# Edge weights of two tiles as one product over 128 partitions: a map stored twice and padded with zeros

## The chip, the core and the metric

The kernel runs on one NeuronCore of a Trainium2 chip. A core has five engines that run on their own and wait for each other by semaphores: TensorE (PE; loads of its stationary operand are shown apart as PEld), VectorE (DVE), ScalarE (ACT), GpSimd (POOL) and SyncE (SP). Tables and inputs lie in HBM; tiles that are worked on lie in SBUF, 128 partitions wide; matrix products are written to PSUM. The metric is the time of one execution on the device in microseconds (us); less is better.

## The reference, cut to what matters

A graph layer over 12,500 nodes with 160 features each and 400,000 edges that are sorted by destination, with a residual and a layer norm. What the change touches is `w`, the weights that each edge gets from its 64 numbers:

```python
h_s = s @ lin1_ws * a * _inv(S_IN)
h_v = jnp.einsum('nci,cd->ndi', v, lin1_wv) * a[:, :, None] * _inv(V_IN)
hid = jax.nn.silu(edge_scalars @ fc_w1 * _inv(R))      # 400000 x 64
w = hid @ fc_w2 * _inv(FC_HID)                          # 400000 x 224
w1, w2, w3, w4, w5 = jnp.split(w, [64, 128, 160, 192], axis=-1)
es = h_s[edge_src]
ev = h_v[edge_src]
...
agg_s = jax.ops.segment_sum(mid_s, edge_dst, num_segments=n) * inv_nn
agg_v = jax.ops.segment_sum(mid_v, edge_dst, num_segments=n) * inv_nn
...
return jnp.concatenate([scalars, gated.reshape(n, 3 * V_OUT)], axis=-1)
...
x = _layernorm(x + _L0_gnn_ref(x, node_vec1, src, dst, edge_attr_4, edge_attr_64, ...))
```

`mid_s` and `mid_v` are products of `w`, of the gathered rows `es` and `ev`, and of the four numbers of the edge. All of it is float32.

## The kernel before, in words

A first part maps all nodes by `lin1` and writes the rows to a table `h_tab` in HBM. Then the edges are worked on in tiles of 128, 3,125 of them. 24 tiles are a chunk, and a chunk has two halves of 12: the first half's edge numbers lie on partitions 0 to 63 of the tile `es`, the second half's on partitions 64 to 127. A step takes a quad of four tiles, two of the one half and two of the other; there are 782 steps (the last one has one tile). The order of the work on every engine is written out by the loop over `steps` (lines 994 to 1063), and each engine takes its instructions in that order.

A step n issues, engine by engine:

- POOL: four gathers of 128 rows each from `h_tab` into `hg` (L476), 160 numbers a row. The third of them carries a wait for the edge weights of step n - 3 (`pace`, lines 1010 and 1011), so that gathers don't run further ahead than that. Six buffers of `hg` are there.
- PE: the edge weights `pw` of the step's four tiles (L551), and then the sums `pa` of step n - 2 (L630), a one-hot product that adds each edge to its destination in a window of 16 nodes; the sums of the two halves go to PSUM partitions 0 to 63 and 64 to 127. In every second step PE also makes `hid` for two later quads (L467: all 128 partitions of `es`, 512 columns), about every third step it turns sums around (L649), about every twelfth it maps them by `lin2` (L664), and for every four tiles of nodes it finishes nodes (L717, L721).
- DVE: the one-hot (L614, written into the free columns of `pw`), the products of `pw` and `hg` (L561, L569), the one-hot times the edge's four numbers (`sel`, L623), and the additions of finished windows into `acc` (L672).
- ACT: the silu of `hid` (L469), and copies out of PSUM.

There are two PSUM buffers of `pw`, two banks each, so the weights of step n wait until DVE has read those of step n - 2.

The edge weights of one tile are a product of `hid` (64 partitions by 128 edges, the stationary operand) and the map `w2` (64 partitions by 224, the moving operand). `w2` stands on partitions 0 to 63 and again on 64 to 127, each half taking the copy on its own partitions. The four products of a quad are issued in the order half 0, half 1, half 0, half 1, so that neighbours lie on different halves of the partitions and write to different PSUM banks. Each float32 product appears in the profile as two loads and two matmuls (6,250 of each for 3,125 tiles).

Lists that are read by slot (`rel`, `eas`) are laid out once in the order in which the quads take their tiles: `by_slots` (L171), `by_slot` (L588), `quads` (L121).

Of the kernel before, what the change touches and what calls it, by code (L numbers as in the profile page):

```python
# [10 lines left out]
F32 = mybir.dt.float32  # L11
# [10 lines left out]
P = 128  # L22
S = 64
# [12 lines left out]
CT = 2 * SIDE  # L36
# [12 lines left out]
NWT = 224  # L49
# [12 lines left out]
def gnn_kernel(  # L62
# [21 lines left out]
    nc = tc.nc  # L84
# [10 lines left out]
    consts = ctx.enter_context(tc.tile_pool(name="consts", bufs=1))  # L95
# [25 lines left out]
    def quads(halves):  # L121
        out = []
        for t in range(0, max(halves), 2):
            out.append([(half, u) for half in range(2) for u in range(t, t + 2) if u < halves[half]])
        return out


# [12 lines left out]
    for c, (_, halves) in enumerate(chunks):  # L140
        for i, slots in enumerate(quads(halves)):
            steps.append((c, i, [(tile_of(c, half, u), half, u) for half, u in slots]))
# [7 lines left out]
    def ahead(t):  # L150
        a0 = t // AHEAD * AHEAD
        if a0 not in aheads:
            n = min(AHEAD, TT - a0)
            idx = loads.tile([P, AHEAD], I32, name="idx")
            eat = loads.tile([P, AHEAD, 4], F32, name="eat", bufs=1)
            k = 0
            while k < n:
                g, u = divmod(a0 + k, GT)
                m = min(n - k, GT - u)
                nc.sync.dma_start(idx[:, k:k + m], src[g][:, u:u + m])  # L160
                nc.sync.dma_start(eat[:, k:k + m].rearrange("p t k -> p (t k)"),
                                  ea[g].rearrange("p t k -> p (t k)")[:, 4 * u:4 * (u + m)])
                k += m
            aheads[a0] = a0, idx, eat
        return aheads[a0]
# [5 lines left out]
    def by_slots(out, of, n, f):  # L171


        m = n // CT
        for u in range(SIDE if m else 0):
            at = u // 2 * 4 + u % 2
            o, i = out[:, at:at + 1], of[:, u:u + 1]
            f(bass.AP(tensor=o.tensor, offset=o.offset,
                      ap=[o.ap[0], [CT * o.ap[1][0], m], [2 * o.ap[1][0], 2], *o.ap[2:]]),
              bass.AP(tensor=i.tensor, offset=i.offset,  # L180
                      ap=[i.ap[0], [CT * i.ap[1][0], m], [SIDE * i.ap[1][0], 2], *i.ap[2:]]),
              u // BT, m)
        return m * CT
# [36 lines left out]
    w1 = consts.tile([2 * S, 2 * S], F32, name="w1")  # L220
    nc.vector.memset(w1, 0.0)

    w2 = consts.tile([2 * S, NWT], F32, name="w2")
    l2 = consts.tile([P, 11, V3], F32, name="l2")
    nc.vector.memset(l2, 0.0)
    share = ends_pool.tile([1, NB], I32, name="share")
# [10 lines left out]
    with tc.tile_pool(name="nodes", bufs=len(starts)) as nodes, tc.tile_pool(  # L237
        name="nodes_ps", bufs=6, space=PSUM
# [33 lines left out]
        for q in range(4):  # L272
            t0, s = divmod(q * QN, P)
            nc.gpsimd.dma_start(at_k[:P - s, q], attr[s:, t0:t0 + NQ])
            if s:
                m = min(NQ, NT - t0 - 1)
# [8 lines left out]
        at = ends_pool.tile([P, NT], F32, name="at")  # L285
# [8 lines left out]
        halves = ends_pool.tile([P, 2], F32, name="halves")  # L294
# [32 lines left out]
        raw = ends_pool.tile([2 * S, NWT], F32, name="raw")  # L327
        for half in range(2):
            r = slice(half * S, (half + 1) * S)
# [14 lines left out]
        for c0, cn, xw, xz in loaded:  # L344
# [7 lines left out]
            n = min(cn, P)  # L352
# [32 lines left out]
    nc.vector.tensor_scalar_mul(half_at, at, 0.5)  # L385
    iota = consts.tile([P, W], F32, name="iota")
    nc.vector.tensor_copy(iota, iota_i)
    at_c = 0
    for a, b in ((64, 128), (0, 64), (192, 224), (160, 192), (128, 160)):
        nc.vector.tensor_scalar_mul(w2[:, at_c:at_c + b - a], raw[:, a:b], 1.0 / math.sqrt(64))  # L390
        at_c += b - a

    scs = consts.tile([S, V3], F32, name="scs")
    nc.sync.dma_start(scs, sc_ws)
# [14 lines left out]
    for to, part, pieces, w, r0, c0, by in maps:  # L409
        for k, piece in enumerate(pieces):  # L410
# [3 lines left out]
            m = terms.setdefault((to, part, four), len(terms))  # L414
            at_r = at_p * V
            r = l2[at_r:at_r + V, m, c0:c0 + w.shape[1]]
# [11 lines left out]
    for t in range(by_slots(rel, dt, TT, relative), TT):  # L428
        nc.vector.tensor_tensor(rel[:, slot_of[t]:slot_of[t] + 1], dt[:, t:t + 1],  # L429
                                lo[:, t // BT:t // BT + 1], op=OP.subtract)  # L430
# [27 lines left out]
    def hidden(pool, psum, es, halves, t0, n):  # L458

        ph = psum.tile([2 * S, Q * P], F32, name="ph", tag="misc")  # L460
        hid = pool.tile([2 * S, Q * P], F32, name="hid", bufs=3)
        ends = [max(0, min(n, m - t0)) for m in halves]
        assert ends[0] >= ends[1]
        for k, c0, c1 in ((2 * S, 0, ends[1]), (S, ends[1], ends[0])):
            if c1 > c0:
                c = slice(c0 * P, c1 * P)
                nc.tensor.matmul(ph[:k, c], w1[:k, :k], es[:k, t0 * P + c0 * P:t0 * P + c1 * P],  # L467
                                 start=True, stop=True)
                nc.scalar.activation(hid[:k, c], ph[:k, c], AF.Silu, scale=1.0 / math.sqrt(64))  # L469
        return hid  # L470
# [73 lines left out]
    weighed, summed = [], []  # L544

    def weights(psum, hid, slots):

        pw = psum.tile([P, Q, 256], F32, name="pw")
        for t, (half, c) in sorted(enumerate(slots), key=lambda k: (k[1][1], k[1][0])):
            r = slice(half * S, (half + 1) * S)  # L550
            weighed.append(nc.tensor.matmul(pw[:, t, :NWT], hid[r, c * P:(c + 1) * P], w2[r],  # L551
                                            start=True, stop=True).ins.name)
        return pw

    def products(pool, pw, hg, n, between=None):
# [32 lines left out]
    def by_slot(t):  # L588

        a0, _, eat = ahead(t)  # L590
        if a0 not in sorted_eat:
            n = min(AHEAD, TT - a0)
            eas = loads.tile([P, AHEAD, 4], F32, name="eas")
            m = n // CT
            for u in range(0, SIDE if m else 0, 2):
                o, i = eas[:, 2 * u:2 * u + 1], eat[:, u:u + 1]
                nc.scalar.copy(
                    bass.AP(tensor=o.tensor, offset=o.offset,
                            ap=[o.ap[0], [4 * CT, m], [4, 2], [8, 2], [1, 4]]),
                    bass.AP(tensor=i.tensor, offset=i.offset,  # L600
                            ap=[i.ap[0], [4 * CT, m], [4, 2], [4 * SIDE, 2], [1, 4]]))
            m *= CT
            for k in range(m, n):
                o = slot_of[a0 + k] - a0
                nc.scalar.copy(eas[:, o], eat[:, k])
            sorted_eat[a0] = eas
        return sorted_eat[a0]
# [172 lines left out]
    with tc.tile_pool(  # L780
        name="fin", bufs=1
    ) as fin, tc.tile_pool(
        name="mine", bufs=2
    ) as mine, tc.tile_pool(
        name="late", bufs=2
    ) as late, tc.tile_pool(name="edge", bufs=2) as edge, tc.tile_pool(
        name="deep", bufs=6
# [199 lines left out]
        with in_order:  # L987
# [6 lines left out]
            for n, (c, i, tiles) in enumerate(steps):  # L994
# [11 lines left out]
                if n == 0:  # L1006
# [61 lines left out]
            n = len(steps)  # L1068
# [29 lines left out]
        with tc.For_i(0, n_redo, 1):  # L1098
# [9 lines left out]
            with tc.For_i(0, n_again, 1) as g, tc.For_i(0, GT, 1) as k:  # L1108
                t = g * GT + k
# [97 lines left out]
```

## Time and profile before

| | |
|---|---|
| median of 3 runs | 4658.97 us (4657.78 to 4659.96) |
| the profiled execution | 4659.28 us, its span 4657.5 us |
| mean granted TensorE clock | 0.870 |
| PE busy | 3852.9 us, 17,955 matmuls |
| PE weight loads | 1891.7 us, 17,955 loads |
| POOL busy | 2995.5 us, of it 2964.8 us in 3,125 gathers |
| DVE busy | 2369.7 us |
| ACT busy | 840.2 us |

The span runs from the first to the last instruction of the core; the execution's own time is 1.8 us longer. In the groups by line, a row gives the line of the kernel, the engine, the operation, what is written and read, its shape and how often; behind the bar stand the busy time, the mean duration of one in ns, and the time that the engine idled just before them, with what ended most of that idle time ("issue": nothing that the profile shows). Busy time of PE is counted with the tail of each matmul, and the next one starts before that tail ends; the chain of work that ended last counts each piece only up to the start of the next.

### The profile page before, as it was taken

The page shows a single profiled execution, that of the slowest core. Times are in us where ns is not written, and L with a number is a line of the kernel's source. Part 1 is how long each engine was busy: PE and PEld are TensorE (multiplying, and loading weights), DVE is VectorE, ACT ScalarE, POOL GpSimd, SP SyncE. Part 2 cuts the span into 40 slices and gives each one's busy share as a digit, 9 for nine tenths or more (in the row PEclk, how much of TensorE's full clock was granted, in tenths as well). Part 3 has the DMA queues.
Part 4 walks back from the last instruction along what each step waited for, and adds up shares of the span by engine and source line. Part 5 has one row for each costly group of instructions (what it writes and reads, how often), then busy time and mean ns, then how long its engine had stood idle before and what let it go on. Part 6 is the DMA issues. An engine that isn't in the chain of part 4 may idle for free.

```text
span 4657.5 us, 53879 instructions
## 1 busy us (share of the span) xinstructions
PE 3852.9 (83%) x17955; PEld 1891.7 (41%) x17955; DVE 2369.7 (51%) x6412; ACT 840.2 (18%) x1872; POOL 2995.5 (64%) x3172
## 2 busy tenths in 40 slices
PE   5788888888888888888888888887888888888886
PEld 4343444444444334344443444343443444444443
DVE  5544554545545455454554555554554554554454
ACT  1211121211111111111111111111111111111112
POOL 6666666666666666666666666666666666666663
PEclk8888898888888898888888888888888898988888
DMA  6333333333333333333333333333333333333331
GB/s 208 93 79 79 95 86 81 94 78 88 95 78 89 87 84 88 90 84 86 90 85 85 89 88 85 89 87 79 93 88 79 93 80 87 95 78 88 86 87 48
DMA packets 237510, 412.26 MB, mean 89 GB/s; under 512 B 78040, under 2 KB 160961, under 8 KB 237093
## 3 DMA queue, kind: packets, MB, share of 16 engines
q0 software_dynamic: 152960, 266.64, 21.8%
q1 hardware_dynamic: 83668, 141.96, 12.5%
q8 instruction: 143, 2.34, 0.2%
q14 instruction: 145, 1.19, 0.1%
q10 hardware_dynamic: 594, 0.13, 0.0%
HBM read 392.49 MB, written 16.00 MB: 88 GB/s over the span
## 4 chain that ended last, share of the span: by engine, by line
PE 63%; issue 12%; another core or an unknown queue 10%; DVE 9%; DMA 2%; POOL 2%; ACT 1%; DVEq 0%; SPq 0%; ACTq 0%; POOLq 0%
PE pa L630 23%; PE pw L551 17%; PE misc L664 8%; PE misc L467 7%; PE misc L649 6%; DVE pr L569 5%; POOL hg L476 2%; PE misc L721 2%; DMA hg<-h_tab,idx 1%; DVE sel L623 1%; PE misc L717 1%; DVE pr L561 1%; DVE pw L614 1%; DMA xz<-in_xv_t_dram 1%
## 5 line engine op out<-in xcount | busy, mean ns | idle before, releaser
L476 POOL DMA_INDIRECT hg<-h_tab,idx x3125 | 2964.8, 949 | 1601.1 <-issue 824.7
L630 PE MATMUL pa<-pr,sel 128*64 128x416 f32 x6250 | 1546.6, 585 | 122.8 <-issue 118.5
L551 PE MATMUL pw<-w,hid 64*128 64x224 f32 x6250 | 1050.7, 408 | 382.9 <-issue 257.7
L614 DVE TENSOR_TENSOR pw<-rel,iota 128x64 f32<-128x64 int16 x782 | 180.1, 230 | 2143.1 <-remote 1114.7
L569 DVE TENSOR_TENSOR pr<-pw,hg 128x384 f32<-128x384 f32 x2346 | 1153.2, 547 | 0.0
L551 PEld LDWEIGHTS pw<-w,hid 64*128 64x128 f32 x6250 | 644.2, 203 | 1078.8 <-issue 742.1
L630 PEld LDWEIGHTS pa<-pr,sel 128*64 128x64 f32 x6250 | 444.4, 149 | 971.3 <-issue 924.5
L561 DVE TENSOR_TENSOR pr<-pw,hg 128x512 f32<-128x512 f32 x782 | 540.2, 691 | 30.3 <-DVE pw L614 1.9
L467 PE MATMUL misc<-es,w 128*128 128x512 f32 (+1 forms) x784 | 491.3, 709 | 30.5 <-DVE rel L429 19.6
L664 PE MATMUL misc<-tt,l 128*96 128x256 f32 (+5 forms) x1496 | 400.3, 411 | 42.8 <-issue 40.6
L469 ACT ACTIVATE hid<-misc 128x512 f32<-128x512 f32 x392 | 234.4, 598 | 977.3 <-remote 277.7
L652 ACT COPY tt<-misc 128x512 f32<-128x512 f32 (+1 forms) x263 | 153.0, 582 | 1426.5 <-remote 826.8
L863 ACT COPY sa<-pa 128x416 f32<-128x416 f32 x521 | 263.9, 507 | 714.2 <-remote 279.9
L649 PE MATMUL misc<-ident,sa 128*128 128x128 f32 (+1 forms) x1558 | 311.3, 290 | 76.6 <-ACT sa L863 42.3
L623 DVE TENSOR_TENSOR sel<-pw,eas 128x256 f32<-128x256 f32 x782 | 323.2, 413 | 0.1
L664 PEld LDWEIGHTS misc<-tt,l 128*96 128x96 f32 (+1 forms) x1496 | 241.9, 176 | 194.9 <-issue 125.9
L649 PEld LDWEIGHTS misc<-ident,sa 128*128 128x128 f32 x1558 | 218.5, 173 | 162.2 <-issue 100.5
L672 DVE TENSOR_TENSOR acc<-acc,os 96x32 f32 x1042 | 194.1, 186 | 53.4 <-remote 16.3
L467 PEld LDWEIGHTS misc<-es,w 128*128 128x128 f32 x784 | 129.3, 205 | 157.3 <-issue 131.7
L649 PE MATMUL misc<-first_last,sa 128*128 128x128 f32 x784 | 188.8, 297 | 4.3 <-issue 4.2
L717 PE MATMUL misc<-ident,acc 96*128 96x96 f32 x196 | 64.0, 332 | 95.7 <-DVE pw L614 68.3
L667 ACT COPY os<-misc 96x512 f32<-96x512 f32 (+2 forms) x68 | 38.4, 564 | 449.9 <-PE misc L664 168.7
(97 smaller groups left out, 852.1 us busy)
## 6 DMA issues: line engine op xcount, KB each, us to landing
es<-in_es_t_dram SPq DMA_DIRECT2D x258, 384.0 KB
hg<-h_tab,idx POOLq DMA_INDIRECT x3125
h_tab<-ht POOLq DMA_DIRECT2D x24, 320.0 KB
xt<-in_x_dram SPq DMA_DIRECT2D x23, 320.0 KB
out_dram<-y SPq DMA_DIRECT2D x23, 320.0 KB
xv<-in_xv_t_dram SPq DMA_DIRECT2D x23, 192.0 KB
eat<-in_ea_dram SPq DMA_DIRECT2D x41, 96.0 KB
xw<-in_xs_t_dram SPq DMA_DIRECT2D x6, 512.0 KB
```

The source lines that it names most:

```text
L467: nc.tensor.matmul(ph[:k, c], w1[:k, :k], es[:k, t0 * P + c0 * P:t0 * P + c1 * P], start=True, stop=True)
L469: nc.scalar.activation(hid[:k, c], ph[:k, c], AF.Silu, scale=1.0 / math.sqrt(64))
L476: got = nc.gpsimd.indirect_dma_start(out=hg[:, t, :], out_offset=None, in_=h_tab, in_offset=bass.IndirectOffsetOnAxis(ap=i, axis=0))
L551: weighed.append(nc.tensor.matmul(pw[:, t, :NWT], hid[r, c * P:(c + 1) * P], w2[r], start=True, stop=True).ins.name)
L561: nc.vector.tensor_mul(two, pw[:, :n, :2 * S].rearrange("p t (k c) -> p t k c", k=2), hg[:, :n, None, :S].to_broadcast([P, n, 2, S]))
L569: nc.vector.tensor_mul(pr[:, :n, first:first + V3].rearrange("p t (i c) -> p t i c", i=3), pw[:, :n, None, 2 * S + k * V:2 * S + (k + 1) * ...
L614: nc.vector.tensor_tensor(oh, rel[:, t0:t0 + n, None].to_broadcast([P, n, W]), iota[:, None, :].to_broadcast([P, n, W]), op=OP.is_equal)
L623: nc.vector.tensor_mul(sel[:, :n], oh[:, :, None, :].to_broadcast([P, n, 4, W]), by_slot(tiles[0][0])[:, u:u + n, :, None].to_broadcast([P ...
L630: summed.append(nc.tensor.matmul(pa[half * ROWS:(half + 1) * ROWS, :NPR], sel[:, t].rearrange("p k w -> p (k w)"), pr, start=start, stop=s ...
L649: nc.tensor.matmul(to.rearrange("p (k b w) -> p k b w", k=kinds, b=n), of, moving, start=True, stop=True, is_transpose=kinds == 4)
L664: nc.tensor.matmul(po[:, k, :nb], l2[r, terms[to, part, four]], a[:, :nb], start=(n == 0), stop=(n == len(of) - 1))
L863: nc.scalar.copy(sa, pas.pop(j)[:, :NPR])
```

## The change

The map `w2` gets a second block of 224 columns: partitions 0 to 63 hold the map in the first block and zeros in the second, partitions 64 to 127 zeros in the first and the map in the second. One product then takes `hid` on all 128 partitions, the tiles of both halves at the same place u, and all 448 columns: its first 224 columns are the weights of the first half's tile, the other 224 those of the second half's. A quad has two such products in place of four. So that the two tiles of a product lie side by side in `pw`, the quad's slots are ordered by place and then by half; before, they were ordered by half. `rel` and `eas` are laid out in that order. The last step, with one tile, uses 64 partitions and 224 columns as before.

```diff
         for t in range(0, max(halves), 2):
-            out.append([(half, u) for half in range(2) for u in range(t, t + 2) if u < halves[half]])
+            out.append([(half, u) for u in range(t, t + 2) for half in range(2) if u < halves[half]])
         return out
...
-    w2 = consts.tile([2 * S, NWT], F32, name="w2")
+    w2 = consts.tile([2 * S, 2, NWT], F32, name="w2")
+    nc.vector.memset(w2, 0.0)
...
-    at_c = 0
-    for a, b in ((64, 128), (0, 64), (192, 224), (160, 192), (128, 160)):
-        nc.vector.tensor_scalar_mul(w2[:, at_c:at_c + b - a], raw[:, a:b], 1.0 / math.sqrt(64))
-        at_c += b - a
+    for half in range(2):
+        r = slice(half * S, (half + 1) * S)
+        at_c = 0
+        for a, b in ((64, 128), (0, 64), (192, 224), (160, 192), (128, 160)):
+            nc.vector.tensor_scalar_mul(w2[r, half, at_c:at_c + b - a], raw[r, a:b], 1.0 / math.sqrt(64))
+            at_c += b - a
...
     def weights(psum, hid, slots):
 
         pw = psum.tile([P, Q, 256], F32, name="pw")
-        for t, (half, c) in sorted(enumerate(slots), key=lambda k: (k[1][1], k[1][0])):
-            r = slice(half * S, (half + 1) * S)
-            weighed.append(nc.tensor.matmul(pw[:, t, :NWT], hid[r, c * P:(c + 1) * P], w2[r],
-                                            start=True, stop=True).ins.name)
+        n = len(slots)
+        for t in range(0, n, 2):
+            half, c = slots[t]
+            m = min(2, n - t)
+            assert half == 0 and all(slots[t + k] == (k, c) for k in range(m))
+            weighed.append(nc.tensor.matmul(
+                pw[:, t:t + m, :NWT], hid[:m * S, c * P:(c + 1) * P], w2[:m * S, :m],
+                start=True, stop=True).ins.name)
         return pw
...
-                            ap=[o.ap[0], [4 * CT, m], [4, 2], [8, 2], [1, 4]]),
+                            ap=[o.ap[0], [4 * CT, m], [8, 2], [4, 2], [1, 4]]),
```

In the loop the order of PE stays, and only the rows of `pw` change. Two steps of PE in the middle of the program, before (`misc` are the PSUM banks for all else, `w_93` is `fc_w1` on the diagonal, `w_95` is `w2`):

```order
L630 MATMUL pa_513<-pr,sel 64x416 x4
L551 MATMUL pw_512<-w_95,hid 128x224 x4
L467 MATMUL misc_515<-es,w_93 128x512
L630 MATMUL pa_513<-pr,sel 64x416 x2
L630 MATMUL pa_514<-pr,sel 64x416 x2
L551 MATMUL pw_511<-w_95,hid 128x224 x4
L649 MATMUL misc_516<-ident,sa 128x128 x2
```

The same place after the change:

```order
L636 MATMUL pa_519<-pr,sel 64x416 x4
L556 MATMUL pw_518<-w_95,hid 128x2x224 x2
L469 MATMUL misc_521<-es,w_93 128x512
L636 MATMUL pa_519<-pr,sel 64x416 x2
L636 MATMUL pa_520<-pr,sel 64x416 x2
L556 MATMUL pw_517<-w_95,hid 128x2x224 x2
L655 MATMUL misc_522<-ident,sa 128x128 x2
```

Four products of 224 columns became two of 448, between the same neighbours; nothing else moved. In the first part, DVE scales the map once more, before the first step (`raw` is the map as loaded, `rel` the destinations relative to their window). Before:

```order
L387 COPY iota<-iota_i 128x16
L390 TENSOR_SCALAR w_95<-raw 128x64 x2
L390 TENSOR_SCALAR w_95<-raw 128x32 x3
L319 MEMSET scv 96x96
L424 TENSOR_TENSOR rel<-dt,lo 128x130x2 x12
```

After:

```order
L387 COPY iota<-iota_i 128x16
L392 TENSOR_SCALAR w_95<-raw 64x64 x2
L392 TENSOR_SCALAR w_95<-raw 64x32 x3
L392 TENSOR_SCALAR w_95<-raw 64x64 x2
L392 TENSOR_SCALAR w_95<-raw 64x32 x3
L319 MEMSET scv 96x96
L426 TENSOR_TENSOR rel<-dt,lo 128x130x2 x12
```

Five scalings over 128 partitions became ten over 64, ahead of the same `rel`. The gathers, the loads, the rows of DVE in the loop and the waits that POOL and DVE carry stand as before.

More of the change, by code (lines that the diff above doesn't have):

```diff
@@ L175, in by_slots @@
         for u in range(SIDE if m else 0):
-            at = u // 2 * 4 + u % 2
-            o, i = out[:, at:at + 1], of[:, u:u + 1]
+            o, i = out[:, 2 * u:2 * u + 1], of[:, u:u + 1]
             f(bass.AP(tensor=o.tensor, offset=o.offset,
-                      ap=[o.ap[0], [CT * o.ap[1][0], m], [2 * o.ap[1][0], 2], *o.ap[2:]]),
+                      ap=[o.ap[0], [CT * o.ap[1][0], m], [o.ap[1][0], 2], *o.ap[2:]]),
               bass.AP(tensor=i.tensor, offset=i.offset,
```

## The prediction

> **What bounds the kernel now.** I read the page first: the busy times, the chain that ended last by engine, and the groups of the lines in question.
>
> ```profile
> PE 3852.9 (83%) x17955; PEld 1891.7 (41%) x17955; DVE 2369.7 (51%) x6412; ACT 840.2 (18%) x1872; POOL 2995.5 (64%) x3172
> PE 63%; issue 12%; another core or an unknown queue 10%; DVE 9%; DMA 2%; POOL 2%; ACT 1%; DVEq 0%; SPq 0%; ACTq 0%; POOLq 0%
> L476 POOL DMA_INDIRECT hg<-h_tab,idx x3125 | 2964.8, 949 | 1601.1 <-issue 824.7
> L551 PE MATMUL pw<-w,hid 64*128 64x224 f32 x6250 | 1050.7, 408 | 382.9 <-issue 257.7
> L551 PEld LDWEIGHTS pw<-w,hid 64*128 64x128 f32 x6250 | 644.2, 203 | 1078.8 <-issue 742.1
> ```
>
> PE is busy for 83% of the span and is 63% of the chain. It is idle for 4657.5 - 3852.9 = 805 us; 382.9 us of that lie just ahead of a `pw` product, and 257.7 us of these wait for nothing that the profile shows ("issue"). So PE is the nearest bound but not an unbroken one. The second candidate is POOL, whose gathers fill 2965 us and which idles 1601 us in between. To see which of the two paces the loop I took stretches of the steady part and compared them. The columns are PE, loads, DVE, ACT, POOL, each busy us with its count of instructions, then the granted clock, the DMA share and GB/s.
>
> ```profile
> 800.00:900.00 100.00, 86.43 (x427) 43.19 (x426) 54.29 (x151) 19.96 (x47) 65.48 (x70) 0.93 0.37 92
> 900.00:1000.00 100.00, 77.09 (x343) 37.53 (x341) 48.21 (x129) 15.37 (x35) 65.68 (x70) 0.84 0.33 83
> 1000.00:2000.00 1000.00, 843.02 (x3899) 408.75 (x3899) 510.57 (x1388) 179.84 (x405) 651.11 (x687) 0.87 0.34 86
> 3000.00:4000.00 1000.00, 834.19 (x3879) 409.17 (x3877) 507.45 (x1379) 177.43 (x402) 650.72 (x687) 0.86 0.34 86
> ```
>
> Two neighbouring stretches of 100 us differ by 84 matmuls and 9.3 us of PE work, and POOL does 70 instructions in both. In whole milliseconds it does 687 in each. PE's extra work thus moves the pace of the gathers little, so an added microsecond on PE need not be one in the time. Where PE works less, its clock is lower too (0.84 against 0.93): part of what it has in hand is lost to a slower clock, and denser work should win some of it back.
>
> **The new product's price.** The chain of waits in the middle of the program, which counts each piece only up to the start of the next:
>
> ```profile
> 2481.11 5.26 PE misc L664 x22
> 2486.36 1.55 PE pa L630 x8
> 2487.91 0.96 PE pw L551 x8
> 2488.87 1.06 PE misc L649 x9
> 2489.93 1.55 PE pa L630 x8
> 2491.47 0.76 PE pw L551 x5
> 2492.24 1.32 issue
> 2493.55 0.66 PE pw L551 x3
> 2494.21 1.05 PE misc L467 x2
> ```
>
> A quad's four products are eight matmuls and take 0.96 us. L664 has products of 256 columns that use the array alone: 5.26 / 22 = 0.239 us each. Two matmuls of 224 columns take 0.96 / 4 = 0.24 us, the same as one of L664: the two halves run beside each other. After the change a quad is two products, four matmuls of 448 columns on all 128 partitions, and nothing runs beside them. By L664 that is 4 x 0.239 x 448 / 256 = 1.67 us; by L467 (512 columns, two in 1.05 us) 4 x 0.525 x 448 / 512 = 1.84 us. No row shows 448 columns. I take 1.70 us, nearer to L664, which is a long run of matmuls as the new ones are. So +0.74 us a quad, and for 781 quads and the last step 782 x 0.74 = +579 us of PE at the clock of those rows. The bounds are 782 x 0.71 = +555 and 782 x 0.88 = +688 us; as the mean clock of the long stretches is 0.87, the 579 us could be 579 / 0.87 = 665 us of the time.
>
> The Trainium skill ("TensorEngine Tiling (Array Packing)", section "Theoretical Speedup") gives up to twice the speed where a contraction of 64 or less is packed two to the array; the change gives this up. By that rule the new quad would cost 2 x 0.96 = 1.92 us, an estimate, and the sum would be 782 x 0.96 = +751 us; the rows above bear it out to 1.67 / 0.96 = 1.74 times.
>
> **What it takes away.** 6250 `pw` matmuls and as many loads become 3126, and PE's 17,955 become 14,831. Busy time of the loads (644.2 us) halves, beside the matmuls, so I cost it at nothing; what hides it is the longer matmul itself. The stalls in front of `pw` are another matter. In the rows above the products of a quad are cut in two by 1.32 us of issue. If such a stall comes with a matmul or load that is issued, half as many cost half: -129 us. The ends are 0 (they belong to the step, not to the instruction) and -258 us (all go).
>
> **Who waits for the products.** The one-hot on DVE (L614) waits for all of the step's weights and is followed by the products (L561, L569) and `sel`; those free `hg` and `pw`. Here each wait has its engine, its tile and its line, then who released it, the us in all, the number of waits and the mean.
>
> ```profile
> DVE pw L614 <- remote: 1114.7, 202, 13.8
> DVE pw L614 <- PE pw L551: 491.8, 167, 8.6
> POOL hg L476 <- issue: 824.7, 2686, 3.2
> POOL hg L476 <- remote: 443.6, 187, 3.1
> POOL hg L476 <- PE pw L551: 146.7, 81, 7.2
> ```
>
> DVE stands still at L614 for 1606 us in these two rows, so weights that come 0.74 us later reach it as a longer wait and not as a queue behind it. Of POOL only 146.7 us are put down to `pw`. The gathers, though, carry the wait for the weights of three steps earlier, and that wait is how more PE work reaches the pace.
>
> ```profile
> 2482.88 0.95 POOL L476 DMA_INDIRECT hg<-h_tab,idx  x1 [1.97 <-remote]
> 2484.13 0.94 POOL L476 DMA_INDIRECT hg<-h_tab,idx  x1 [0.30 <-issue]
> ```
>
> The first gather here stood 1.97 us, about where PE began its 5.26 us of L664, and the next one 0.30 us. 1.97 / 5.26 = 0.37 of a block of extra PE work shows as a pause of the gathers, by one place; the stretches of 100 us, where 9.3 us show as none, are the other end. I take 0.37, because the new work comes in every step and not now and then.
>
> **The edits ahead of the loop.** The scaling of the map on DVE, and what is behind it:
>
> ```profile
> 45.61 0.46 DVE w L390 x5
> 46.07 0.10 DVE scv L319
> 46.16 13.31 issue
> 70.74 0.96 PE pw L551 x8
> ```
>
> Ten scalings over 64 partitions take 0.92 us where five took 0.46; the 13.31 us behind them, in which the chain waits for nothing shown, hide that, and if that cover is gone it is +0.5 us. The memset of 448 columns is bounded by none and by 0.94 us, that of the other memset (128 x 1056) among the first instructions, where nothing is due. The first two quads stand on the chain: 2 x 0.74 = +1.5 us. The slots' new order moves ACT's copies of `eas` and the copies of `rel` at equal counts and sizes: 0, hidden by ACT's 82% of idle time.
>
> **The sum.** 579 - 129 = +450 us of PE, of which 0.37 shows: +167 us, and +1.5 us at the start. On the profiled execution's 4659.28 us (its span 4657.5 and 1.8 around it; 0.01% above the median of the runs, 4658.97) this gives 4828, rounded to 4830 us. In this case's own range, nothing more than the hidden end is 4668; the dear end, three quarters of the 450 us, is 5000.
>
> **Rivals.**
>
> *PE sets the end throughout* (chance 0.20). For it: PE is 83% busy and 63% of the chain, and the added work would bring it near 100%. Against: 687 in every millisecond whatever PE does. Then +665 - 129 = +536: 5195 us, and with the price by L467 about 688 / 0.87 - 129 = +662: 5320.
>
> *The gathers pace it, and all is hidden* (0.07). For: the two stretches of 100 us. The added 579 us would fit PE's 805 idle us. Against: the pause of 1.97 us. The time would stay within 0.2% (4650 to 4668 us), which is about what a measurement of this kernel can tell from no change.
>
> *Faster: fewer instructions on PE let it run ahead* (0.33). PE's queue handles half as many `pw` instructions, the stalls of 257.7 us go in half or in full, the clock of 0.84 in thin stretches rises to 0.93, and the wait that the gathers carry is answered earlier. The place is the break inside the quad at 2492.24; the price is -129 to -258 us if the added work lies wholly in PE's idle time: 4530 to 4401 us. It decides from the point where less than 129 of the 579 us show, a share of 0.22, which lies between the two ends above. Against: POOL would have to work faster than 687 a millisecond, and the chain has 1.55 us of `pa` in every step, which the change leaves. Below 4000 it can't go: 3125 gathers at the pace of the two rows above (2484.13 - 2482.88 = 1.25 us) are 3906 us, and the loop begins about 50 us into the span and ends about 40 before its end:
>
> ```profile
> L476 POOL DMA_INDIRECT hg<-h_tab,idx x3125: 942/949/1125, 51.3 to 4613.1; - x196
> ```
>
> The Trainium skill ("Perfetto Trace Analysis", section "Matmuls") says that larger matmuls are more efficient than smaller ones when possible; by that rule this rival would win. The trace agrees only in part: it has the stalls ahead of small products, but a pair of them costs no more than one of L664.
>
> **How the numbers follow.** Forecast 0.40, then 0.20, 0.07 and 0.33. Slower is 0.40 + 0.20 = 0.60, same 0.07, faster 0.33. The range goes from 4450, which cuts off about 0.06 of the faster case (three quarters of the stalls gone and more), to 5200, which cuts off half of the PE-bound case and a little besides, 0.12.
>
> **What the profile after would show.** The row of `pw` has 3126 matmuls and 3126 loads of 128 partitions with 448 columns, and a quad takes 1.7 us on the chain; under 1.5 or over 1.9, the price was wrong. PE has 14,831 matmuls, and its loads are busy some 300 us less. Idle time by issue ahead of `pw` is near 129 us; if it is still 250, the stalls belong to the step. POOL falls from 687 in a millisecond to 687 x 4659 / 4830 = 663; 687 means the hidden case, more than 690 the faster one, 616 the PE-bound one. The clock of the long stretches rises above 0.87 if PE is denser.
>
> **What would make it wrong.** The share of 0.37 rests on one pause; it is the least certain number. If the gathers are held by PE's lateness, and not by its work, fewer instructions may bring the release forward by more than the added columns delay it, and then the sign turns.

## The result and the profile after

The changed kernel takes 4633.28 us (median of 5 runs, 4628.95 to 4641.42) against 4659.96 us of the kernel before beside it: ratio 0.9945 (0.9932 to 0.9958), 0.55% faster. The forecast was 4830 us and slower. The profiled execution has a span of 4631.5 us.

The rows of the page that answer to those shown of the kernel before (busy times, the chain by engine, the gathers, the products of the edge weights and their loads, the sums):

```profile
PE 3917.8 (85%) x14831; PEld 1791.3 (39%) x14831; DVE 2367.2 (51%) x6418; ACT 834.6 (18%) x1872; POOL 2987.9 (65%) x3172
PE 51%; another core or an unknown queue 21%; DVE 14%; issue 8%; ACT 2%; DMA 2%; POOL 1%; DVEq 0%; SPq 0%; ACTq 0%; POOLq 0%
L478 POOL DMA_INDIRECT hg<-h_tab,idx x3125 | 2957.3, 946 | 1583.8 <-issue 829.6
L556 PE MATMUL pw<-w,hid 128*128 128x448 f32 x3126 | 1463.7, 591 | 231.9 <-DVE pr L575 119.1
L636 PE MATMUL pa<-pr,sel 128*64 128x416 f32 x6250 | 1385.8, 557 | 60.5 <-issue 51.9
L556 PEld LDWEIGHTS pw<-w,hid 128*128 128x128 f32 x3126 | 558.7, 199 | 1093.5 <-issue 742.8
```

The instruction counts are as expected: 3126 products of 448 columns, 14,831 matmuls. Products of the edge weights are busy 413 us longer than before (1463.7 for 1050.7), yet PE as a whole only 65 us (3917.8 for 3852.9), in the main because the clock is higher (0.923 against 0.870): the sums, which didn't change, take 557 ns each where they took 585. PE's idle time fell from 805 to 714 us (4631.5 - 3917.8), and none of its added work shows in the time. The chain now spends 21% on "another core or an unknown queue" where it spent 10%.

The time can be read from POOL almost alone. Its gathers are busy 2957 us (before 2965), and its idle time ahead of gathers fell from 1601.1 to 1583.8 us: together -25 us, and the span is shorter by 26. Whole milliseconds, in the columns of the prediction, and the waits (us in all, number of waits, the longest one):

```profile
1000.00:2000.00 1000.00, 860.73 (x3225) 391.79 (x3225) 513.03 (x1399) 183.16 (x416) 652.25 (x690) 0.93 0.35 87
2000.00:3000.00 1000.00, 851.60 (x3197) 386.01 (x3195) 504.96 (x1374) 175.62 (x401) 651.13 (x689) 0.92 0.34 86
```

```profile
DVE pw L620 <- remote: 1193.9, 179, 9.5
POOL hg L478 <- issue: 829.6, 2666, 4.9
POOL hg L478 <- remote: 445.2, 177, 3.4
DVE pw L620 <- PE pw L556: 349.7, 102, 8.5
POOL hg L478 <- PE pw L556: 109.8, 52, 6.1
PE pw L556 <- issue: 35.2, 33, 4.9
```

POOL does 689 or 690 instructions in a millisecond (687 before). The time between two gathers by issue (829.6) is nearly what it was (824.7); the pauses beyond it are 1583.8 - 829.6 = 754 us (before 1601.1 - 824.7 = 776). This split is rough: one wait by issue lasted 4.9 us, and other releasers are also named for ordinary gaps of 0.30 us. Counted one by one in the traces, gaps of more than 0.6 us between two gathers are 328 before, 2.27 us each in the mean, and 279 after, 2.54 us each: the change made the pauses fewer, not shorter. So the question of this study is what the pauses are. A place in the timeline shows one (columns: start, duration, engine, line; in brackets the idle time before and its releaser):

```profile
2495.26 0.95 POOL L478 DMA_INDIRECT hg<-h_tab,idx  x1 [0.30 <-issue]
2495.59 1.77 PE L556 MATMUL pw<-w,hid 128*128 128x448 f32 x4
...
2496.51 0.95 POOL L478 DMA_INDIRECT hg<-h_tab,idx  x1 [0.30 <-issue]
2499.86 0.51 ACT L869 COPY sa<-pa 128x416 f32<-128x416 f32 x1 [3.03 <-remote]
2499.86 0.23 DVE L620 TENSOR_TENSOR pw<-rel,iota 128x64 f32<-128x64 int16 x1 [7.72 <-remote]
2500.10 0.94 POOL L478 DMA_INDIRECT hg<-h_tab,idx  x1 [2.64 <-remote]
```

PE's last product ends at 2497.36 in the record. ACT, DVE and POOL, which all wait for work of PE, start within 0.24 us of each other, 2.5 to 2.7 us later, 2.4 us after the end of the last gather (2497.46), and the profile finds no releaser. Twelve gathers ran 0.30 us apart ahead of that pause. I call this *late updates*: what PE has done becomes known to the others long after its record ends, mostly once the gathers have stopped. The Trainium skill ("Perfetto Trace Analysis", section "Per-engine timelines") says that PE's update is pushed only when PSUM has acknowledged the writes, and that PE's end in a profile is computed and not observed. So the trace can't tell whether the update or the work itself was late; both are meant by the word here.

### The profile page after: what moved, and what is told of

It is laid out like the page before. It is cut to its first block, busy times and chain, and to the rows that moved or that the text cites. A ratio compares the mean times of both kernels' runs of the same rounds, so it can differ in the third digit from the quotient of the medians.

```text
span 4631.5 us, 47652 instructions
## 1 busy us (share of the span) xinstructions
PE 3917.8 (85%) x14831; PEld 1791.3 (39%) x14831; DVE 2367.2 (51%) x6418; ACT 834.6 (18%) x1872; POOL 2987.9 (65%) x3172
## 4 chain that ended last, share of the span: by engine, by line
PE 51%; another core or an unknown queue 21%; DVE 14%; issue 8%; ACT 2%; DMA 2%; POOL 1%; DVEq 0%; SPq 0%; ACTq 0%; POOLq 0%
PE pw L556 18%; PE pa L636 16%; DVE pr L575 9%; PE misc L670 7%; PE misc L469 4%; PE misc L655 4%; DVE sel L629 2%; PE misc L727 2%; DVE pr L567 1%; DVE pw L620 1%; POOL hg L478 1%; DVE acc L678 1%; PE misc L723 1%; DMA xz<-in_xv_t_dram 1%
## 5 line engine op out<-in xcount | busy, mean ns | idle before, releaser
L478 POOL DMA_INDIRECT hg<-h_tab,idx x3125 | 2957.3, 946 | 1583.8 <-issue 829.6
L556 PE MATMUL pw<-w,hid 128*128 128x448 f32 x3126 | 1463.7, 591 | 231.9 <-DVE pr L575 119.1
L636 PE MATMUL pa<-pr,sel 128*64 128x416 f32 x6250 | 1385.8, 557 | 60.5 <-issue 51.9
L556 PEld LDWEIGHTS pw<-w,hid 128*128 128x128 f32 x3126 | 558.7, 199 | 1093.5 <-issue 742.8
L636 PEld LDWEIGHTS pa<-pr,sel 128*64 128x64 f32 x6250 | 407.9, 143 | 806.8 <-issue 752.5
L469 PE MATMUL misc<-es,w 128*128 128x512 f32 (+1 forms) x784 | 420.7, 616 | 101.5 <-ACT tt L658 57.8
L670 PE MATMUL misc<-tt,l 128*96 128x256 f32 (+5 forms) x1496 | 377.4, 401 | 72.9 <-issue 42.1
L655 PE MATMUL misc<-ident,sa 128*128 128x128 f32 (+1 forms) x1558 | 290.6, 277 | 98.6 <-ACT sa L869 48.2
L655 PEld LDWEIGHTS misc<-ident,sa 128*128 128x128 f32 x1558 | 232.8, 170 | 234.4 <-issue 168.8
L469 PEld LDWEIGHTS misc<-es,w 128*128 128x128 f32 x784 | 149.1, 194 | 272.3 <-issue 189.3
L655 PEld LDWEIGHTS misc<-first_last,sa 128*128 128x128 f32 x784 | 111.2, 152 | 7.2 <-issue 7.2
```

What stands on the lines that cost most here:

```text
L478: got = nc.gpsimd.indirect_dma_start(out=hg[:, t, :], out_offset=None, in_=h_tab, in_offset=bass.IndirectOffsetOnAxis(ap=i, axis=0))
L556: weighed.append(nc.tensor.matmul(pw[:, t:t + m, :NWT], hid[:m * S, c * P:(c + 1) * P], w2[:m * S, :m], start=True, stop=True).ins.name)
L636: summed.append(nc.tensor.matmul(pa[half * ROWS:(half + 1) * ROWS, :NPR], sel[:, t].rearrange("p k w -> p (k w)"), pr, start=start, stop=s ...
L655: nc.tensor.matmul(to.rearrange("p (k b w) -> p k b w", k=kinds, b=n), of, moving, start=True, stop=True, is_transpose=kinds == 4)
L670: nc.tensor.matmul(po[:, k, :nb], l2[r, terms[to, part, four]], a[:, :nb], start=(n == 0), stop=(n == len(of) - 1))
```

## Experiments

Theories: A, the gathers pace the loop, with pauses that belong to the kernel's waits, and PE's added work is hidden; B, the halved number of PE instructions makes the gain; C, PE paces it, and smaller stalls pay for the added columns; D, the pauses are PE's late updates. The edits are to the changed kernel unless another is named. All ratios are to the kernel before on the same chip at the same time.

**Added or removed work, on a first chip.** Three edits of `weights` (the products split in two, the first one issued twice, both issued twice), and one that leaves out a gather:

```diff
+            for k in range(m):
-                pw[:, t:t + m, :NWT], hid[:m * S, c * P:(c + 1) * P], w2[:m * S, :m],
+                pw[:, t + k, :NWT], hid[:m * S, c * P:(c + 1) * P], w2[:m * S, k],
```

> The changed kernel, but each product over 128 partitions split in two of 224 columns: the same columns on PE as after the change, and the 6250 products' matmuls of before. Theory A (the gathers pace the loop, what PE does below about 5.8 us a step is hidden): the time stays at that of the changed kernel, 4620 to 4650 us. Theory B (the gain of 0.55% comes from the halved number of PE instructions, and the added columns are hidden): 4660 us or more. Theory C (PE paces it, and the halved stalls pay for the added columns): 4633 plus 100 to 260 us.

```diff
+            for _ in range(2 if t == 0 else 1):
```

> The changed kernel with the first of the two products of a quad issued twice: +0.85 us of PE a step (782 x 0.85 = 665 us in all), some 5.5 us a step at full clock. Theory A: hidden, as 5.5 is still below the 5.8 us of a step: 4630 to 4720 us. Theory C: 4633 + 665 = 5300 us.

```diff
+            for _ in range(2):
```

> The changed kernel with both products of a quad issued twice: +1.70 us of PE a step (1330 us in all), some 6.4 us a step at full clock. Theory A: now PE is the bound, 782 x 6.4 = 5000 and about 100 us around the loop: 5050 to 5200 us. Theory C: 4633 + 1330 = 5960 us.

```diff
-        for t, i in enumerate(idx):
+        for t, i in enumerate(idx[:3]):
...
+        if n == Q:
+            hg = bass.AP(tensor=hg.tensor, offset=hg.offset, ap=[hg.ap[0], [106, Q], [1, D]])
```

> The changed kernel without the fourth gather of every quad (the products read the rows of the other three with a shorter stride, so the sums are of other numbers): 2343 gathers and the same work on PE, DVE and ACT. Theory A: three steps take 9 x 1.25 + 2.6 = 13.9 us in place of 17.3, and PE with 4.7 us a step comes to be the bound at about the same: 3650 to 4000 us. Theory C: 4600 to 4640 us, since PE's work is unchanged.

The surprise was the kernel before: 4001.5 us here (median of 15, 3999.92 to 4011.03), where 4660 stood. Four padded products took 4002.48 us (ratio 1.0003, 0.9994 to 1.0012), one product twice 4214.12 (1.0529, 1.0512 to 1.0545), both twice 4798 and three gathers 3628 (one run each). Four padded products there, the page, a stretch and the timeline:

```profile
PE 3696.6 (92%) x17955; PEld 2329.1 (58%) x17955; DVE 2368.6 (59%) x6418; ACT 869.0 (22%) x1872; POOL 2989.6 (75%) x3172
L478 POOL DMA_INDIRECT hg<-h_tab,idx x3125 | 2959.0, 947 | 957.3 <-issue 800.0
```

```profile
2000.00:3000.00 1000.00, 937.35 (x4527) 587.75 (x4526) 593.92 (x1618) 218.91 (x477) 756.58 (x800) 0.96 0.43 101
```

```profile
2488.36 1.78 PE L557 MATMUL pw<-w,hid 128*128 128x224 f32 x8
...
2490.18 0.23 DVE L621 TENSOR_TENSOR pw<-rel,iota 128x64 f32<-128x64 int16 x1 [0.35 <-PE pw L557]
```

The gathers are as long as ever (947 ns), but the pauses beyond issue are 957.3 - 800.0 = 157 us in place of 754, and even these are ordinary gaps: from the first gather to the last no gap is longer than 0.63 us. POOL does 800 instructions in a millisecond, one every 1.25 us, and DVE starts 0.04 us after PE's products end (2490.14). No wait of this run is put down to a remote releaser. Here updates are prompt, and the time is what the prediction named as the floor of the gathers, 4000 us. So theory A held in its core (gathers pace it, 579 us of added PE work are hidden) and not in what the pauses are. With the gathers' load taken down by a quarter PE is the bound, and with PE's load taken up it is again. From the chains, start, duration and piece:

```profile
2484.60 1.70 PE pw L556 x4
2486.30 0.86 PE misc L469 x2
2487.16 1.55 PE pa L638 x8
```

```profile
2492.93 2.45 PE pw L557 x6
```

```profile
2485.64 3.20 PE pw L557 x8
```

These are the chains with three gathers, with one product twice and with both. With three gathers PE works without a gap, and a quad's two products take 1.70 us, the price that the prediction took. (This kernel leaves out a quarter of the gathers; its 3628 us lie just under the 3650 to 4000 that were expected.) Both products twice against one twice are 584 us apart (4798 - 4214), 0.75 us a product where they stand in a row. Both doubled kernels came out below what was expected: one product twice (4214 for 4630 to 4720) because the pauses that held the time up in the record are not there, both twice (4798 for 5050 to 5200) because a step takes (4798 - 95) / 782 = 6.0 us and not 6.4. With 95 us around the loop, as in the floor, three gathers take 4.5 us a step and one product twice 5.3; each is 2.8 us and the products (1.70, 2.45 and 3.20 us on the chain).

**Which chip, and the gathers' wait.** The two kernels again, and both without the wait on the third gather of a step:

```diff
-                    deep, [index(t) for t, _, _ in tiles], {2: weighed_by[n - 3] if n >= 7 else None})
+                    deep, [index(t) for t, _, _ in tiles], {})
```

> The kernel before, unchanged, for a profile on the chip on which the experiments run. In the comparisons so far this chip took 4001.5 us for it where 4659 us stood in the record. Theory D (on the first chip the semaphore updates of PE came late while gathers ran, and the pauses of the gathers are that lateness): here the pauses of about 2 us are gone, gathers follow each other every 1.25 us, 800 in a millisecond, and no wait is put down to a remote or unknown releaser. Theory A in its first form (the pauses belong to the kernel's own waits): the pauses are still there, and something else in the gathers is shorter.

> The changed kernel, unchanged, timed against the kernel before on this chip. Theory A and D (gathers pace it, 3125 x 1.25 + 95 = 4001 us is their floor): 3998 to 4010 us if the chip is like the last, ratio 1.000; on a chip with late updates 4633 to 4660 us, ratio 0.994. Theory B (half as many instructions of PE save time by themselves): ratio 0.994 on either. Theory C (PE paces it): over 1.02 where the stalls are gone.

> The changed kernel without the wait that the third gather of a step carries for the weights of three steps earlier; what holds the gathers then is their six buffers alone. Theory D: on a chip where PE's updates are prompt the wait holds nothing, 3998 to 4010 us; where they are late, the pauses go elsewhere, 4600 us or more. Theory A in its first form: with the wait gone the pauses go, 4001 us on either chip.

> The kernel before without that wait. Theory D: 4001 us where PE's updates are prompt; 4650 us or more where they are late. Theory A in its first form: 4001 us on either chip.

This was another chip, and updates were late on it: the kernel before 4707.69 us, the changed one 4673.46 (0.9931, 0.9917 to 0.9944). Without the wait the changed kernel takes 5047.69 us (1.0718, 1.0701 to 1.0734), the kernel before 5119 (one run). Of the kernel before, the changed kernel, and the changed one without the wait, the gathers' row, in this order:

```profile
L476 POOL DMA_INDIRECT hg<-h_tab,idx x3125 | 2955.8, 946 | 1661.5 <-issue 827.9
```

```profile
L478 POOL DMA_INDIRECT hg<-h_tab,idx x3125 | 2957.6, 946 | 1623.0 <-issue 831.5
```

```profile
L478 POOL DMA_INDIRECT hg<-h_tab,idx x3125 | 2959.1, 947 | 1994.9 <-DVE pr L575 1059.8
```

Idle time of the gathers fell by 38.5 us with the change, and the span by 38.0 (4709.6 to 4671.6): the gain is time in which the gathers pause. Again the pauses are fewer (gaps over 0.6 us: 371 of 2.20 us in the mean before, 302 of 2.50 us after). Without the wait, gathers run on until their six buffers are full and then wait for DVE, which waits for PE: pauses are as long as 6.75 us in the place shown, after a run of 12 or more:

```profile
2500.05 0.94 POOL L478 DMA_INDIRECT hg<-h_tab,idx  x1 [0.30 <-issue]
2507.75 0.99 POOL L478 DMA_INDIRECT hg<-h_tab,idx  x1 [6.75 <-DVE pr L575]
```

A wait in the kernel thus keeps the price of the late updates down; theory A in its first form, by which the pauses would go with the wait, falls.

**Instructions or columns.** Under late updates the four padded products and the doubled product were run again beside the changed kernel, with one more form of the wait:

```diff
-                    deep, [index(t) for t, _, _ in tiles], {2: weighed_by[n - 3] if n >= 7 else None})
+                    deep, [index(t) for t, _, _ in tiles], {2: weighed_by[n - 3] if n >= 7 and n % 3 == 0 else None})
```

> The four products of 224 columns over 128 partitions again (the columns of the changed kernel, the 6250 matmuls of before). Where PE's updates are prompt: 4002 us again, ratio 1.000. Where they are late: if the gain of the change comes from the number of PE instructions that queue up while updates are held, ratio 1.000 or over to the kernel before; if it comes from the denser work of PE at a higher clock, the ratio of the changed kernel, 0.993 to 0.995.

> The changed kernel, unchanged, beside the others. Where PE's updates are prompt (the kernel before at 4001 us): 3998 to 4010 us, ratio 1.000, all 579 us of added PE work hidden. Where they are late: ratio 0.993 to 0.995, as measured before.

> The changed kernel with the first product of each quad issued twice, +0.85 us of PE a step. Prompt: 4214 us again, PE the bound. Late: PE has 5.1 us a step at full clock against 5.9 us a step of the loop; if the gathers and their pauses set the pace there, the time moves by less than 150 us from the changed kernel's (4630 to 4820 us), if PE does, by 600 us.

> The changed kernel with the gathers' wait in every third step alone. Prompt: 4002 us, nothing waits. Late: if each run of gathers costs one pause of 2.5 us whatever its length, and runs come to be of 12 throughout, three steps take 12 x 1.25 + 2.6 = 17.6 us, 4590 us and about 60 around it: 4600 to 4660 us, as the changed kernel or a little less; if longer runs bring longer pauses, as without the wait, up to 5000 us.

Then two kernels that change the number of PE instructions, and a last form of the wait:

```diff
+            nc.tensor.matmul(pw[:, t, :8], hid[:m * S, c * P:(c + 1) * P], w2[:m * S, 0, :8],
+                             start=True, stop=True)
             weighed.append(nc.tensor.matmul(
```

> The changed kernel with one more product of 8 columns ahead of each of its products (it is overwritten by the product itself): PE has 17,957 matmuls and as many loads again, as before the change, and hardly more columns. Where PE's updates are late: if the number of PE instructions makes the gain, the ratio to the kernel before goes back to 1.000 (0.998 to 1.003); if not, it stays at 0.993 to 0.995. Where they are prompt: 4002 us.

```diff
-                add_tile(pas[j], half, sel, slot, pr[:, slot], start=(m == 0), stop=stop)
+                if m % 2 == 0 or stop:
+                    add_tile(pas[j], half, sel, slot, pr[:, slot], start=(m == 0), stop=stop)
```

> The changed kernel without a third of the one-hot sums (the second tile of each window of three is left out of its sum): 12,750 matmuls on PE in place of 14,831. Late updates: if the number of PE instructions counts, as much again as the change brought for its 3124, 2083 / 3124 x 0.65% = 0.4% below the changed kernel, ratio to before about 0.989; if it was something else, 0.993 to 0.995 as the changed kernel. Prompt: 4002 us.

```diff
-                    deep, [index(t) for t, _, _ in tiles], {2: weighed_by[n - 3] if n >= 7 else None})
+                    deep, [index(t) for t, _, _ in tiles], {0: weighed_by[n - 3] if n >= 7 else None})
```

> The changed kernel with the gathers' wait for the weights of three steps earlier on the first gather of a step and not on the third, so that a run of gathers ends two earlier. Since longer runs (no wait, or one in three steps) took 3.5 to 7% longer where updates are late, shorter ones may gain: 0.98 to 0.995 of the kernel before; if a pause of about 2 us is paid for each run whatever its length, more pauses: 1.00 to 1.03. Prompt: 4002 to 4020 us.

> The changed kernel, unchanged, beside these. Late: ratio 0.993 to 0.995. Prompt: 1.000, 3998 to 4010 us.

All of these met late updates (the kernel before took 4713 us beside the first four and 4664 beside the last). By the number of PE's matmuls (the loads are as many); pauses are the gathers' idle time less that by issue, and the last column is the profiled run's clock:

| kernel | matmuls | columns of `pw` a quad | ratio (95%) | pauses, us | clock |
|---|---|---|---|---|---|
| fewer_sums | 12,749 | 4 x 448 | 0.9903 (0.9888 to 0.9919) | 713 | 0.875 |
| after_fourth | 14,831 | 4 x 448 | 0.9935 (0.9920 to 0.9950) | 737 | 0.925 |
| after_third | 14,831 | 4 x 448 | 0.9936 (0.9922 to 0.9949) | 777 | 0.916 |
| one_product_twice_2 | 16,395 | 6 x 448 | 0.9998 (0.9989 to 1.0008) | 814 | 0.971 |
| before | 17,955 | 8 x 224, in pairs | 1 | 776 to 834 | 0.87 |
| four_padded_2 | 17,955 | 8 x 224, alone | 1.0007 (0.9998 to 1.0016) | 823 | 0.920 |
| tiny_products | 17,957 | 4 x 448 and 4 x 8 | 1.0048 (1.0035 to 1.0062) | 811 | 0.941 |

Four padded products do the work of the changed kernel, at nearly its clock, with the instructions of the kernel before, and the gain is gone. Tiny products add hardly any columns but the instructions, and the gain is gone and a little more. Fewer sums take 2082 matmuls away, with their columns, and gain another 0.3%, close to the 0.4% expected, at the lowest clock but one of the table; by the gathers' idle time in all they are level with the changed kernel beside them (1567.7 and 1570.6 us), so where these 14 us lie isn't clear. One product twice adds 0.85 us a quad, some 665 us, and costs 4712.02 - 4682.00 = 30 us beside the changed kernel. So under late updates the number of PE instructions moves the time, with the columns equal (four padded products against the changed kernel), and the clock doesn't. Matmuls and loads change together in all these kernels, so which of the two counts is not shown. That columns cost nothing at all is not shown either: one product twice adds half of the matmuls that the change took away, and loses the whole gain where by count alone half of it would be left. The new order of the slots by itself is ruled out as the cause of the gain, since the four padded products have it too. Pauses compare on one chip: fewer_sums, after_fourth and tiny_products were on one, after_third, one_product_twice_2 and four_padded_2 on another, and on each the kernels with more matmuls than the changed one have the larger pauses. It is their number that grows (gaps over 0.6 us again): 299 for after_third, 338 for one_product_twice_2, 383 for four_padded_2; 286 for after_fourth, 349 for tiny_products. The small steps between kernels of equal count (0.4% from four padded to tiny products) and between 16,395 and 17,955 are not explained.

The gathers' rows of the changed kernel (after_third) and of the four padded products (four_padded_2), on one chip, are those of the main comparison:

```profile
L478 POOL DMA_INDIRECT hg<-h_tab,idx x3125 | 2957.7, 946 | 1627.6 <-issue 850.2
L478 POOL DMA_INDIRECT hg<-h_tab,idx x3125 | 2964.7, 949 | 1659.9 <-issue 836.5
```

The gathers' row and one of PE's, of fewer sums and then of tiny products (on one chip), carry the two ends of the table:

```profile
L478 POOL DMA_INDIRECT hg<-h_tab,idx x3125 | 2955.6, 946 | 1567.7 <-issue 854.6
L636 PE MATMUL pa<-pr,sel 128*64 128x416 f32 x4168 | 1015.7, 582 | 111.4 <-ACT sa L869 75.3
```

```profile
L478 POOL DMA_INDIRECT hg<-h_tab,idx x3125 | 2955.3, 946 | 1634.2 <-issue 823.2
L556 PE MATMUL pw<-w,hid 128*128 128x8 f32 x3126 | 541.8, 242 | 154.4 <-issue 88.7
```

How an instruction can count and its width not is seen in the kernel before, in a stretch of its timeline where gathers have run for a while:

```profile
2505.36 0.13 PEld L630 LDWEIGHTS pa<-pr,sel 128*64 128x64 f32 x1 [1.29 <-issue]
2506.77 0.51 PE L630 MATMUL pa<-pr,sel 128*64 128x416 f32 x1 [1.62 <-issue]
2507.48 0.16 PEld L630 LDWEIGHTS pa<-pr,sel 128*64 128x64 f32 x1 [1.99 <-issue]
2508.20 0.85 PE L630 MATMUL pa<-pr,sel 128*64 128x416 f32 x1 [0.92 <-issue]
```

Loads of 0.13 us and matmuls of 0.51 us start at distances of 0.71, 1.41 and 0.72 us: PE passes one instruction each 0.7 us (with one missing in the record), long or short. Tiny products show it with widths that are far apart:

```profile
2747.19 0.17 PE L556 MATMUL pw<-w,hid 128*128 128x8 f32 x1 [0.45 <-issue]
2747.89 0.19 PEld L558 LDWEIGHTS pw<-w,hid 128*128 128x128 f32 x1 [1.13 <-issue]
2748.59 0.54 PE L558 MATMUL pw<-w,hid 128*128 128x448 f32 x1 [1.23 <-issue]
2749.29 0.19 PEld L558 LDWEIGHTS pw<-w,hid 128*128 128x128 f32 x1 [1.22 <-issue]
```

A product of 8 columns, a load and a product of 448 columns each keep the next instruction back for 0.70 us. Counted in the whole traces, steps of 0.6 to 0.8 us from the start of one load or matmul to the next, three or more in a row, number 275 in the kernel before and 40 in the changed kernel, 64 and 225 in after_third and four_padded_2, and none in the four padded products under prompt updates. So these stretches go with the number of instructions and with late updates. That they make the gain is argued, not shown, and the count doesn't order every kernel: one product twice has only 83 and lost the gain, fewer sums have 100 and took the least time.

The other forms of the wait: in every third step 4848.2 us (1.0291, 1.0265 to 1.0317), against an expected 4600 to 4660 if a pause cost the same whatever the run; longer runs bring longer pauses. On the first gather of a step 4632.05 us (0.9932, 0.9917 to 0.9947), the same as the changed kernel beside it (4632.19), so no gain from shorter runs. The changed kernel on two more chips:

> The changed kernel, unchanged, in the hope of a chip on which the kernel before takes 4001 us. Prompt updates: 3998 to 4010 us, ratio 1.000 with all added PE work hidden. Late ones: ratio 0.993 to 0.995 again.

> The changed kernel, unchanged, once more. Where PE's updates are prompt (the kernel before at 4001 us): 3998 to 4010 us, ratio 1.000. Late: ratio 0.993 to 0.995.

Both met late ones: 0.9941 (0.9925 to 0.9958) and 0.9927 (0.9911 to 0.9944). With prompt updates the changed kernel itself has therefore not been timed; the four padded products, which do the same work with more instructions, stood at 1.0003 there. The new order of the slots without the padded product was not tried.

Under late updates only fewer sums took less time than the changed kernel, and they leave out a third of the sums.

## Why the prediction was wrong

- *What bounds the kernel.* "PE is the nearest bound but not an unbroken one" was wrong; the two stretches of 100 us and the 687 instructions in every millisecond said so, and the forecast gave them too little weight. The gathers and their pauses set the time under late updates, the gathers alone under prompt ones.
- *The price of a quad, 1.70 us.* Right where PE works without a gap: the chain of three gathers shows 1.70. The rule of the Trainium skill on packed products ("TensorEngine Tiling (Array Packing)", section "Theoretical Speedup"), up to twice, would have given 1.92 (an estimate); the measured gain of packing is 1.70 / 0.96 = 1.77 times.
- *The step that failed is the share of 0.37 by which added PE work was to show.* One product twice measures it: 30 us for 665, 0.05, and these 30 us came with 1564 more instructions. Four padded products, with +579 us of columns at an unchanged count, give +0.07% or 3 us, a share under 0.01. What moved the time in place of PE's work was the number of its instructions, and with it the number and the total of POOL's pauses. The pause of 1.97 us at the long L664 is better read as one of the pauses between runs of gathers; that it fell on the block was read as a cause. The kernel before shows that it wasn't:

```profile
2481.04 5.33 PE L664 MATMUL misc<-tt,l 128*96 128x256 f32 x22
2482.64 0.23 DVE L614 TENSOR_TENSOR pw<-rel,iota 128x64 f32<-128x64 int16 x1 [6.42 <-remote]
2482.69 0.60 ACT L469 ACTIVATE hid<-misc 128x512 f32<-128x512 f32 x1 [3.76 <-remote]
```

DVE, ACT and this gather (2482.88) start within 0.24 us of each other, 3.5 us before the block ends at 2486.37. The forecast's last sentence had named this case: gathers held by PE's lateness, and not by its work, and then the sign turns.
- *The stalls ahead of `pw`, -129 us.* By issue they fell from 257.7 to 35.2 us, more than half, and with the 6250 products of four_padded_2 they are back at 191.2, so they come with the instructions. But most of them are not on the path: the whole gain is 25 to 40 us of POOL's time.
- *The waits.* The last number of the rows of waits was called their mean; it is the longest one. The mean of the first row is 1114.7 / 202 = 5.5 us and not 13.8. The sum doesn't use these numbers.
- *The loads.* Expected some 300 us less, measured 100 (1891.7 to 1791.3): the loads of two halves had run beside each other too (6250 x 203 ns is 1269 us, in 644 us of busy time).
- *The rivals.* The faster one had the sign and the mechanism, fewer instructions, and its floor of 4000 us was met to 0.1% by the kernel before where updates were prompt. Its size was off: it priced the stalls of PE (-129 to -258 us), and the time fell by 26 us. "Wholly hidden" was right of the columns to within the share above, and left out what fewer instructions gain. "PE sets the end" held only where a gather was left out or a product doubled under prompt updates.
- *The clock* rose as said, 0.870 to 0.923, and bought nothing that shows: four_padded_2 had 0.920 and gained nothing.

## What to carry to other kernels

Where one engine's instruction count per millisecond is the same in every stretch whatever the others do, price a change by what it does to that engine's pauses, and count an added load elsewhere as hidden until that engine's pauses move. Where several engines start at nearly the same instant after a pause, with no releaser shown, look at what they waited for before the pause is priced by whatever PE happened to run beside it. Under such pauses fewer, wider PE instructions are worth having even when they cost more columns: the same columns in half as many instructions were 0.7% (4716.9 to 4682.0 us), which agrees with the Trainium skill's sentence on larger matmuls ("Perfetto Trace Analysis", section "Matmuls").

## What the runs showed of the hardware

The same program, the kernel before, took 4001.5 us in the first comparison of the experiments and 4659 to 4713 us in all others. The four padded products were profiled in both states, with spans of 4000.2 and 4718.6 us: their gathers are busy 2959.0 and 2964.7 us (947 and 949 ns each) and idle 957.3 and 1659.9 us, so nearly the whole difference lies in pauses between runs of gathers. In the pause shown above, ACT, DVE and POOL start 2.5 to 2.7 us after the record of PE's last product ends; with prompt updates DVE starts 0.04 us after it. Which of the two is met does not come from the kernel, and nothing in these runs tells what it comes from. It need not be the chip: the chip of the first comparison has the number 7, and so has that of the comparison with the tiny products some 35 minutes later, where the kernel before took 4664 us; whether the two are one chip is not known. While gathers run on under late updates, PE passes through stretches of one instruction each 0.7 us; whether that is a cause of the late updates or another face of the same thing stays open.
